# Four chained graph layers on one core: the new-state gate's state side as seven block products, SiLU as one ScalarE function, and a schedule search with other durations

## The chip, the cores and the metric

The kernel runs on one core of a Trainium2 chip. The metric is the device time of one execution in microseconds (us), taken as the median of several executions. All data are float32. The core has one engine for matrix products (TensorE, "PE" in the profile; its weight loads are shown apart as "PEld"), three engines for elementwise work (VectorE "DVE", ScalarE "ACT", GpSimd "POOL") and a queue for transfers (SyncE "SP"). The engines run beside each other and wait for one another by semaphores.

## The reference, cut to what matters

The input x has 128 graphs of 64 nodes with 256 features. Four layers follow one another; each adds its result to x and normalises the sum.

```python
def gru(m, h):                                    # layer 0, five rounds
    gi, gh = m @ w_ih.T + b_ih, h @ w_hh.T + b_hh
    r = sigmoid(i_r + h_r); z = sigmoid(i_z + h_z)
    n = tanh(i_n + r * h_n)                       # n: the candidate; h_n: state's side of it
    return (1 - z) * n + z * h
for l in range(5):
    agg = A.T @ (h @ weight[l]);  h = gru(agg, h)
x = layernorm(x + h * mask)

agg = epsilon * x + adj @ x                       # layer 1
hid = silu(rmsnorm(agg @ W1 + b1) * rms_weight)
x = layernorm(x + hid @ W2 + b2)

x = layernorm(x + project(expmap0(adj @ logmap0(x))))   # layer 2: artanh (a logarithm), tanh

h = x @ W_w.T + W_b; a = softmax-like(exp(h @ a1 + h @ a2) * adj)   # layer 3
x = layernorm(x + a @ h)
```

## The kernel before: the parts that the change and the steps touch

The 128 graphs are taken in 16 groups of 8 (`NG = 16`), so a group has 512 columns of features (`R = 512`), cut in two halves of 256 (`HR = 256`). The 256 features are two blocks of 128 (`KD = 2`), one for each set of 128 partitions. All instructions of all groups are first only listed, each with an engine, an assumed duration and what it reads and writes. A search (`Flow`, `Plan`) then plays several orders through, with up to four groups under way at once, keeps the best plan, and issues the instructions in that order. Some copies may go to either ScalarE or VectorE (`either`, `copied`, `scaled`); the search picks the engine. The order on each engine is then fixed, and the chip's engines wait for semaphores where the plan's times do not hold.

One round of layer 0 for one group:

```python
def sides(n):                                      # for each half n
    ...                                            # transposes of h, aggregate -> agg (p_agg)
    p_hn = bank("p_hn")
    product(p_hn, w_hn, lambda k: h[:, k, half(n)], True, True, (h, n))   # 4 matmuls of 256 columns
    for c in range(KD):                            # evict with the bias, either engine
        scaled(300, hnb[:, c, half(n)] <- p_hn[:, c*HR:(c+1)*HR], 0.5, half_b...)

sides(0)
product(p1, a11[l], agg half 0); copied(420, uu <- p1)
product(p_in[0], w_in[l], agg half 0)
product(p1, a12, h half 0); tanh_half(ur <- p1)
new_n(0, ur)
p_a2 = sides(1)
minus(t1, a2, of(a, 0)); minus(t2, of(h, 1), t1)    # 4 VectorE instructions, 128x512
minus(t3, of(h, 1), a2); minus(t4, t2, of(h, 0))
product(pu, s2[l], t2); plus(uu, pu, uu)
product(pv, s3[l], t3); plus(uv, pv, uu)
product(pw, s1[l], t1); product(pv, na22, t4); plus(uv, pw, uv); plus(uz, pv, uu)
product(pw, s4[l], h half 1); ...
product(p_in[1], w_in[l], agg half 1); ...
```

The gates r and z for both halves are a 2x2 by 2x2 product of blocks (blocks: agg or h, gate r or z, half 0 or 1). It is done with seven block products in place of eight: `a11`, `a12`, `s1` to `s4`, `na22` are sums and differences of weight blocks, `t1` to `t4` those of the data. A block product here is four matmuls. The candidate's two sides, `w_in` on agg and `w_hn` on h, are plain: eight matmuls each for both halves.

Layer 1's activation, with `half_r` half of `rms_w` and `w2s` scaled by `rms_w` once at the start:

```python
for c in range(KH):                                # 8 chunks of 128x512 in each group
    dve: v = (v + b1) * ps_r
    act: th = tanh(half_r * v)
    dve: v = (th + 1) * v
```

The search's assumptions:

```python
pe:  {512: 0.86, 256: 0.435, 128: 0.23, 1: 0.21} us
dve: 0.16 + 0.00105 * n    act: 0.27 + 0.00077 * n     pool(us)
act(2600, ... AF.Ln ...)                           # the logarithm with its table loads, as a long operation
```

Of the kernel before, what the change touches and what calls it, by code (L numbers as in the profile page):

```python
# [16 lines left out]
P = 128  # L17
# [25 lines left out]
class Op:  # L43
    __slots__ = ("eng", "us", "run", "ways", "stream", "n", "kb", "need", "then", "bufs", "opens", "id", "way")

    def __init__(self, ways, stream, n, kb):
        self.ways = {eng: (us, run) for eng, us, run in ways}
        self.eng, self.us, self.run = ways[0]
        self.stream, self.n, self.kb = stream, n, kb
        self.need, self.then, self.bufs, self.opens, self.id, self.way = 0, [], (), None, 0, 0.0  # L50


class Plan:


    def __init__(self, flow):
# [10 lines left out]
        self.past, self.order = None, []  # L67

    def copy(self):
# [6 lines left out]
        c.past, c.order = (self.past, self.order), []  # L76
        return c

    def advance(self, until, rank):
# [3 lines left out]
        while self.left and clock["PE"] < until:  # L83
            best = None
            for s in range(self.first, min(self.first + flow.WINDOW, len(self.queues))):
                for e, q in self.queues[s].items():
                    opened = False
                    for _, o in zip(range(flow.AHEAD[e]), q):
# [10 lines left out]
                        key = (t + o.ways[e][0] - min(w[0] for w in o.ways.values()) if len(o.ways) > 1 else t, *rank(s, o))  # L99
# [4 lines left out]
            _, o, eng, t = best  # L104
            for e in o.ways:
                self.queues[o.stream][e].remove(o)
# [37 lines left out]
class Flow:  # L144
# [13 lines left out]
    HOPS = {"from PE": 0.25, "to PE": 0.3, "else": 0.1}  # L158
# [3 lines left out]
    TRANSFERS = 8  # L162
    WINDOW, STRETCH, WIDTH, LAG = 4, 25.0, 8, 40.0
# [13 lines left out]
    def op(self, eng, us, run, w=(), r=(), kb=0):  # L177
        self.either([(eng, us, run)], w, r, kb)

    def either(self, ways, w, r, kb=0):  # L180

        o = Op(ways, len(self.streams) - 1, len(self.ops), kb)
# [31 lines left out]
    def hop(self, e, to):  # L214
        if e == to:
            return 0.0
        return self.HOPS["from PE" if e == "PE" else "to PE" if to == "PE" else "else"]

# [42 lines left out]
def kernel(  # L261
# [82 lines left out]
    def act(n, run, w, r):  # L344
        flow.op("ACT", 0.27 + 0.00077 * n, run, w, r)
# [72 lines left out]
    def gate_w(name):  # L418
        return fixed([P, KD, D], name)

    a12, na22, w_hn = gate_w("a12"), gate_w("na22"), gate_w("w_hn")
    a11, s1, s2, s3, s4, w_in = ([gate_w(f"{n}_{l}") for l in range(L)] for n in ("a11", "s1", "s2", "s3", "s4", "w_in"))
# [6 lines left out]
    half_b, half_r = fixed([P, NV], "half_b"), fixed([P, KH], "half_r")  # L429
# [36 lines left out]
    flow.op("ACT", 1.5, lambda: nc.scalar.activation(warm, one4, AF.Tanh))  # L466
# [23 lines left out]
    dve(4, lambda: nc.vector.tensor_scalar(half_r.tile(), cols[:, 2 * NV + KH:], 0.5, None, OP.mult), [half_r], [cols])  # L490
# [13 lines left out]
    def hh_out(i, k, ps):  # L504
        if i == 0:
            dve(256, lambda: nc.vector.tensor_copy(a12[:, k, :], ps[:, :D]), [(a12, k)], [ps])
            dve(256, lambda: nc.vector.tensor_scalar(na22[:, k, :], ps[:, D:], -1.0, None, OP.mult), [(na22, k)], [ps])
        else:
            dve(256, lambda: nc.vector.tensor_copy(w_hn[:, k, :], ps[:, :D]), [(w_hn, k)], [ps])
# [10 lines left out]
    for l in range(L):  # L520
# [9 lines left out]
        a21 = unit("AB"[l % 2], S, f"a21_{l}", (P, KD, D))  # L530
        for k in range(KD):
            for i, n in ((0, 2 * D), (1, D)):
# [5 lines left out]
                for dst, at in (((a11[l], 0), (a21, D)) if i == 0 else ((w_in[l], 0),)):  # L538
                    act(256, lambda ps=ps, k=k, dst=dst, at=at: nc.scalar.copy(dst[:, k, :], ps[:, at:at + D]),
                        [(dst, k)], [ps])  # L540

        def sums(e, us, l=l, a21=a21):
            v = nc.vector if e == "DVE" else nc.gpsimd
            for o, x0, x1 in ((s1[l], a21, na22), (s2[l], s1[l], a11[l]), (s3[l], a11[l], a21), (s4[l], a12, s2[l])):
                flow.op(e, us, lambda o=o, x0=x0, x1=x1: v.tensor_sub(o.tile(), x0.tile(), x1.tile()), [o], [x0, x1])
        sums("DVE", 0.7) if l == 0 else sums("POOL", 1.32)
# [5 lines left out]
    m11, m12, mn22, ms1, ms2, ms3, ms4 = range(7)  # L552
# [34 lines left out]


    for k in range(KH):
        act(256, lambda k=k: nc.scalar.activation(w2s[:, k, :], w2s[:, k, :], AF.Identity, scale=rmsc(k)), [(w2s, k)], [(w2s, k), cols])  # L590
# [21 lines left out]
    def group(g):  # L612
# [104 lines left out]
        def gated(l, h):  # L717
# [5 lines left out]
            def sides(n):  # L723
# [5 lines left out]
                p_agg = aggregate(agg, hr, 2 * n, n)  # L729
                p_hn = bank("p_hn")  # L730
                product(p_hn, w_hn, lambda k: h[:, k, half(n)], True, True, (h, n))
                for c in range(KD):
                    scaled(300, lambda c=c: hnb[:, c, half(n)], lambda c=c: p_hn[:, c * HR:(c + 1) * HR], lambda: 0.5,
                           lambda c=c: half_b[:, 2 * KD + c:2 * KD + c + 1], [(hnb, (n, c))], [p_hn, half_b])
                return p_agg
# [3 lines left out]
            t1, t2, t3, t4 = (tA, 0), (tA, 1), (tB, 0), (tB, 1)  # L739
            a = agg  # L740

            def view(t):
                return t[0][:, t[1] * KD:(t[1] + 1) * KD, :]

            def minus(o, x0, x1, r):
                dve(512, lambda: nc.vector.tensor_sub(view(o), x0(), x1()), [o], r)  # L746

            def of(t, n):
                return lambda: t[:, :, half(n)]

            def k_of(t, n):
# [351 lines left out]
```

## Time and profile before

| | before |
|---|---|
| time, median of 3 (lowest to highest) | 2431.12 us (2430.6 to 2432.45) |
| span of the profiled execution | 2430.5 us |
| PE busy | 2394.7 us, 12258 matmul records |
| PEld busy | 2102.9 us |
| DVE busy | 1893.4 us |
| ACT busy | 1147.1 us |
| POOL busy | 188.2 us |
| HBM traffic | 25.74 MB read, 8.39 MB written |

A line of the profile's groups reads: source line, engine, operation, what it writes and reads by the program's names, shapes, the number of records; then the busy time in us and the mean duration of one in ns; then the time for which the engine stood idle just before such instructions, and who ended that. One float32 matmul instruction leaves two records: `p_hn`, for instance, has 16 x 5 x 8 = 640 instructions in the program and 1280 records. As matmuls overlap in the pipeline, the mean duration of one record is longer than the distance between two.

### The profile page before, as it was taken

Reading aid. Unit: us, or ns where it says so; the run is one execution under the profiler, and the core shown is the slowest. Engines: PE = TensorE matmul, PEld = TensorE weight load, DVE = VectorE, ACT = ScalarE, POOL = GpSimd, SP = SyncE. Lnnn points to the kernel's source line nnn. Section 1 sums busy time; section 2 is a strip of 40 time slices with the busy share of each in tenths; the row PEclk is TensorE's granted clock in tenths of the full one; section 3 lists DMA queues with packets and bytes.
Section 4 is the critical chain, followed back from the end, with each engine's and each line's share of the span. In section 5 each row is a group of like instructions: output and inputs, shape, how many; then the busy total and the mean of one; then the engine's idle time right before and its main releaser. Section 6 shows DMA issues by size and latency. Waiting matters only on the chain.

```text
span 2430.5 us, 32703 instructions
## 1 busy us (share of the span) xinstructions
PE 2394.7 (99%) x12258; PEld 2102.9 (87%) x12258; DVE 1893.4 (78%) x4097; ACT 1147.1 (47%) x2408; POOL 188.2 (8%) x144
## 2 busy tenths in 40 slices
PE   9999999999999999999999999999999999999995
PEld 7888888888888888888888888888888888888864
DVE  3668787887888877778777887888787787878777
ACT  4434544444444444454444545455444544445453
POOL 4000000000100000000000100000000000000011
PEclk9999999999999999999999999999999999999997
DMA  4000000000000000000000000000000000000000
GB/s 127 3 1 12 1 29 1 18 12 1 29 1 27 3 18 11 1 27 3 16 14 1 29 1 27 3 19 11 1 29 1 18 12 1 27 9 18 9 9 18
DMA packets 39725, 36.21 MB, mean 15 GB/s; under 512 B 9956, under 2 KB 38656, under 8 KB 39568
## 3 DMA queue, kind: packets, MB, share of 16 engines
q1 hardware_dynamic: 37840, 32.25, 4.2%
q8 instruction: 97, 1.59, 0.3%
q10 hardware_dynamic: 1328, 1.31, 0.2%
q0 software_dynamic: 400, 0.57, 0.1%
q14 instruction: 60, 0.49, 0.1%
HBM read 25.74 MB, written 8.39 MB: 14 GB/s over the span
## 4 chain that ended last, share of the span: by engine, by line
PE 94%; DVE 4%; ACT 1%; DMA 1%; issue 0%; POOL 0%; SPq 0%; POOLq 0%; ACTq 0%; DVEq 0%
PE p_v L663 11%; PE p_w L663 11%; PE p_in L663 11%; PE p_r L663 11%; PE p_hn L663 11%; PE ps_o L333 9%; PE ps_agg L333 6%; PE p_u L663 6%; PE ps_hr L643 3%; PE ps_a L333 2%; PE p_wh L882 2%; PE p_vh L882 2%; PE p_1h L882 2%; PE ps_T L633 1%; PE ps_att L333 1%; PE p_uh L882 1%
## 5 line engine op out<-in xcount | busy, mean ns | idle before, releaser
L663 PE MATMUL p_hn<-hT,w_hn 128*128 128x256 f32 x1280 | 322.8, 380 | 0.0
L663 PE MATMUL p_in<-agg,w_in 128*128 128x256 f32 x1280 | 315.4, 379 | 0.0
L663 PEld LDWEIGHTS p_in<-agg,w_in 128*128 128x128 f32 x1280 | 240.2, 190 | 31.1
L663 PEld LDWEIGHTS p_hn<-hT,w_hn 128*128 128x128 f32 x1280 | 227.9, 191 | 22.7
L333 PE MATMUL ps_o<-w2s,hid 128*128 128x256 f32 x1024 | 231.2, 379 | 0.0
L333 PEld LDWEIGHTS ps_o<-w2s,hid 128*128 128x128 f32 x1024 | 193.9, 190 | 27.3 <-issue 1.2
L678 POOL TENSOR_TENSOR rstd<-ve,pow 128x4 f32<-128x4 f32 (+1 forms) x64 | 82.5, 1289 | 1491.6 <-DVE ve L676 1484.0
L767 ACT ACTIVATE V<-V,half_b 128x256 f32<-128x256 f32 x160 | 72.7, 500 | 199.2 <-DVE V L763 199.0
L663 PE MATMUL p_u<-tA,s 128*128 128x256 f32 x640 | 158.1, 381 | 1.4 <-DVE tA L746 0.6
L663 PE MATMUL p_w<-tA,s 128*128 128x256 f32 x640 | 158.1, 379 | 0.0
L663 PE MATMUL p_r<-hT,a 128*128 128x256 f32 x640 | 156.9, 379 | 0.0
L663 PE MATMUL p_r<-agg,a 128*128 128x256 f32 x640 | 156.7, 379 | 0.0
L663 PE MATMUL p_v<-tB,s 128*128 128x256 f32 x640 | 155.4, 379 | 0.0
L663 PE MATMUL p_v<-tB,na 128*128 128x256 f32 x640 | 154.5, 379 | 0.0
L663 PE MATMUL p_w<-hT,s 128*128 128x256 f32 x640 | 154.3, 379 | 0.0
L349 ACT COPY agg<-ps_agg 128x512 f32<-128x512 f32 x154 | 89.9, 584 | 114.2 <-PE ps_agg L333 98.8
L333 PEld LDWEIGHTS ps_agg<-edge,hr 128*128 128x128 f32 x1024 | 136.1, 191 | 6.6
L354 ACT ACTIVATE hnb<-p_hn,half_b 128x256 f32<-128x256 f32 x232 | 101.6, 472 | 81.4 <-PE p_hn L663 67.4
L333 PE MATMUL ps_agg<-edge,hr 128*128 128x128 f32 x1024 | 138.8, 275 | 0.0
L663 PEld LDWEIGHTS p_u<-tA,s 128*128 128x128 f32 x640 | 119.3, 190 | 21.0 <-DVE tA L746 2.3
L663 PEld LDWEIGHTS p_v<-tB,s 128*128 128x128 f32 x640 | 120.9, 190 | 16.3 <-PE ps_att L333 0.2
L663 PEld LDWEIGHTS p_w<-hT,s 128*128 128x128 f32 x640 | 120.7, 190 | 16.0
(233 smaller groups left out, 4686.5 us busy)
## 6 DMA issues: line engine op xcount, KB each, us to landing
x<-in_x_dram SPq DMA_DIRECT2D x16, 512.0 KB, 3.6
xr<-in_x_dram SPq DMA_DIRECT2D x16, 512.0 KB, 3.6
out_dram<-x_n SPq DMA_DIRECT2D x16, 512.0 KB, 2.9
edge<-in_adj_dram SPq DMA_DIRECT2D x32, 64.0 KB, 2.3
wm<-in_L_gnn_weight_dram SPq DMA_DIRECT2D x5, 256.0 KB, 5.3
w2s<-in_L_gnn_W_dram SPq DMA_DIRECT2D x1, 1024.0 KB, 10.0
w<-in_L_gnn_W_dram SPq DMA_DIRECT2D x2, 512.0 KB, 3.5
w_in_L_gnn_w_hh_dram<-in_L_gnn_w_hh_dram ACTq DMA_DIRECT2D x1, 512.0 KB, 5.2
```

What stands on the lines that cost most here:

```text
L333: return nc.tensor.matmul(o, lhsT, rhs, start=(k == 0), stop=(k == nk - 1))
L349: flow.either([("ACT", 0.27 + 0.00077 * n, lambda: nc.scalar.copy(o(), i())), ("DVE", 0.16 + 0.00105 * n, lambda: nc.vector.tensor_copy(o( ...
L354: flow.either([("ACT", 0.27 + 0.00077 * n, lambda: nc.scalar.activation(o(), i(), AF.Identity, bias=bias(), scale=scale())), ("DVE", 0.16 ...
L633: turn(lambda j=j, c=c: nc.tensor.transpose(ps[:, c * HR + j * P:c * HR + (j + 1) * P], src[:, 2 * n + j, c * P:(c + 1) * P], ident.tile() ...
L643: turn(lambda j=j, c=c: nc.tensor.transpose(ps[:, j * D + c * P:j * D + (c + 1) * P], src[:, c, (2 * n + j) * P:(2 * n + j + 1) * P], iden ...
L663: pe(256, lambda c=c, k=k: nc.tensor.matmul(ps[:, c * HR:(c + 1) * HR], w[:, k, c * P:(c + 1) * P], v(k), start=first and c == k == 0, sto ...
L678: pool(1.1, lambda: nc.gpsimd.tensor_tensor(rstd[:, :m, :], ve[:, :m, :], pow2[:, :m, :], OP.pow), [rstd], [ve])
L767: act(256, lambda c=c: nc.scalar.activation(o[:, c, :], src(c), AF.Tanh, bias=half_b[:, i * KD + c:i * KD + c + 1], scale=0.5), [(o, c)], ...
L882: pe(256, lambda c=c: nc.tensor.matmul(ps[:, c * HR:(c + 1) * HR], w1f[:, w, (2 * q + c) * P:(2 * q + c + 1) * P], v[0](), start=first and ...
```

## The change

There are three parts.

**State's side of the candidate.** `h @ w_hn` for both halves is itself made a 2x2 by 2x2 product (blocks: input features 0 or 1, output features 0 or 1, half 0 or 1) with seven block products, each of one matmul of 256 columns. It needs the four data sums `t1` to `t4` of h over features and halves. So that the gates can share them, the gates' product is cut in the same way: its blocks are now input features 0 or 1, and each block product takes h's part and agg's part one after the other into the same bank (`gate`). The sums are now made for h and for agg apart, each 128x256.

```diff
-            def sides(n):
+            def agg_of(n):
                 ...
-                p_hn = bank("p_hn")
-                product(p_hn, w_hn, lambda k: h[:, k, half(n)], True, True, (h, n))
-                for c in range(KD):
-                    scaled(300, lambda c=c: hnb[:, c, half(n)], ...)
+            def sums(x, i):
+                for o, x0, x1 in ((of(t1), at(0, 1), at(0, 0)), (of(t2), at(1, 1), of(t1)),
+                                  (of(t3), at(1, 1), at(0, 1)), (of(t4), of(t2), at(1, 0))):
+                    dve(256, ... nc.vector.tensor_sub(o[0](), x0[0](), x1[0]()) ...)
+            def gate(ps, m, v, first, last):
+                for i, w in ((1, w_h), (0, w_a[l])):
+                    for c in range(KD):
+                        pe(256, ... nc.tensor.matmul(ps[:, c * HR:(c + 1) * HR], w[:, m, c * P:(c + 1) * P], v[i][0](), ...))
+            def state_side():
+                px, py = bank("p_hx"), bank("p_hy")
+                prod(px, 0, m11, block(0, 0), True)
+                copied(256, su[0], lambda: px[:, :HR], ...)
+                prod(px, 0, m12, block(1, 0))
+                scaled(256, out(0, 0)[0], lambda: px[:, :HR], lambda: 1.0, lambda: b(0), ...)
+                prod(px, 1, ms2, sum_of(t2));        plus(su, px, 1, su)
+                prod(py, 0, ms3, sum_of(t3), True);  plus(sv, py, 0, su)
+                prod(py, 1, ms1, sum_of(t1))
+                prod(py, 0, mn22, sum_of(t4))
+                plus(out(0, 1), py, 0, su, 1);       plus(out(1, 1), py, 1, sv, 1)
+                prod(py, 1, ms4, block(1, 1));       plus(out(1, 0), py, 1, su, 0)
...
-            sides(0)
-            product(p1, a11[l], k_of(a, 0), True, False, (a, 0))
+            agg_of(0)
+            gate(p1, m11, block(0, 0), True, False)
             copied(420, lambda: uu.tile(), lambda: blocks_of(p1.tile()), [uu], [p1])
-            product(p_in[0], w_in[l], k_of(a, 0), True, True, (a, 0))
-            product(p1, a12, k_of(h, 0), False, True, (h, 0))
+            gate(p1, m12, block(1, 0), False, True)
             tanh_half(ur, ...)
+            sums(h, 1)
+            state_side()
+            product(p_in[0], w_in[l], lambda k: agg[:, k, half(0)], True, True, (agg, 0))
             new_n(0, ur)
-            p_a2 = sides(1)
-            minus(t1, ...); minus(t2, ...); minus(t3, ...); minus(t4, ...)
-            product(pu, s2[l], k_view(t2), True, True, t2)
+            agg_of(1)
+            sums(agg, 0)
+            gate(pu, ms2, sum_of(t2), True, True)
             plus(uu, pu, uu)
             ...                                    # pv, pw in the same way
```

The weights' sums are made once at the start, in the same blocks (`w_h`, `w_hn`, and `w_a` for each round); for rounds 1 to 4 on GpSimd as before.

**Layer 1's activation.** ScalarE's SiLU function takes the place of the tanh and of one VectorE instruction, and the scaling of `w2s` at the start goes.

```diff
-            th = u("VZR"[c % 3], f"th{c}")
-            act(512, ... nc.scalar.activation(th.tile(), v, AF.Tanh, scale=half_r[:, c:c + 1]) ...)
-            dve(512, ... nc.vector.scalar_tensor_tensor(v, th.tile(), 1.0, v, OP.add, OP.mult) ...)
+            act(512, lambda v=v, c=c: nc.scalar.activation(v, v, AF.Silu, scale=rmsc(c)), parts, [*parts, cols], SILU)
...
-    for k in range(KH):
-        act(256, ... w2s[:, k, :] = w2s[:, k, :] * rmsc(k) ...)
```

**The search.** It now knows which function tables ScalarE holds (`sets`: tanh with exp or with SiLU, exp, the logarithm and SiLU each in their own), adds a load where the table changes, prefers ScalarE for a copy that either engine can take unless VectorE is earlier by a margin, and has some other durations.

```diff
+    TANH, EXP, LN, SILU = ("exp", "silu"), ("exp",), ("ln",), ("silu",)
+    TABLE = 1.28
+    SOONER = 0.4
+                        elif o.sets and self.table not in o.sets:
+                            t += flow.TABLE
-                        key = (t + o.ways[e][0] - min(w[0] for w in o.ways.values()) if len(o.ways) > 1 else t, *rank(s, o))
+                        key = (t + flow.SOONER if len(o.ways) > 1 and e == "DVE" else t, *rank(s, o))
-    HOPS = {"from PE": 0.25, "to PE": 0.3, "else": 0.1}
+    HOPS = {"from PE": 0.25, "to PE": 0.3, "else": 0.1, "own": 0.0}
-        act(2600, lambda: nc.scalar.activation(fac.tile(), fac.tile(), AF.Ln), [fac], [fac])
+        act(4, lambda: nc.scalar.activation(fac.tile(), fac.tile(), AF.Ln), [fac], [fac], LN)
-        dve(800, onto_ball, [th, un], [th, un, urn])
+        dve(900, onto_ball, [th, un], [th, un, urn])
```

## Prediction

> **What bounds the kernel now.** I read the shares of the engines first, then the slices, then PE's waits stretch by stretch, and last the chain of work that ended last. The page opens with these lines:
>
> ```profile
> PE 2394.7 (99%) x12258; PEld 2102.9 (87%) x12258; DVE 1893.4 (78%) x4097; ACT 1147.1 (47%) x2408; POOL 188.2 (8%) x144
> PE   9999999999999999999999999999999999999995
> DVE  3668787887888877778777887888787787878777
> PE 94%; DVE 4%; ACT 1%; DMA 1%; issue 0%; POOL 0%; SPq 0%; POOLq 0%; ACTq 0%; DVEq 0%
> ```
>
> PE is busy in every slice but the last, and 94% of the chain is PE. A table by stretches (span, then PE, PEld, DVE, ACT and POOL busy) tells where its 35.8 us of idle time lie:
>
> ```profile
> 0.00:61.00 61.00, 57.60 (x277) 43.77 (x278) 21.80 (x54) 24.86 (x60) 26.23 (x32) 1.00 0.43 127
> ...
> 2300.00:2370.00 70.00, 66.03 (x270) 45.51 (x270) 52.65 (x90) 38.84 (x68) 8.57 (x5) 0.98 0.03 8
> 2370.00:2431.00 61.00, 34.97 (x146) 28.33 (x144) 46.80 (x188) 23.80 (x58) 10.01 (x8) 0.77 0.05 18
> 300.00:2300.00 2000.00, 1997.29 (x10343) 1773.35 (x10342) 1600.54 (x3441) 953.30 (x2001) 134.73 (x93) 1.00 0.04 13
> ```
>
> The start leaves 3.4 us, the last 130 us leave 29.5, and the 2000 us in between only 2.7, although VectorE has 80% of that stretch to do. So in the middle time is PE work and nothing else; at the end it is a chain of small operations. The unit of PE work is read from the timeline, where groups of eight records (four instructions) of 256 columns begin 1.72 to 1.73 us apart:
>
> ```profile
> 1212.05 1.89 PE L663 MATMUL p_u<-tA,s 128*128 128x256 f32 x8
> 1213.77 1.89 PE L663 MATMUL p_v<-tB,s 128*128 128x256 f32 x8
> 1215.50 1.03 PE L663 MATMUL p_w<-tA,s 128*128 128x256 f32 x4
> ```
>
> One matmul instruction of 256 columns is therefore 0.432 us, not the 380 ns of a record's mean, as records overlap.
>
> **What the Trainium skill says.** "Perfetto Trace Analysis", section "Identifying the Most-Contended Engine", warns that matmul busy time is a bad measure of the distance to the roofline, as pipelined matmuls look smaller, and points to the weight loads' share. Here that is 87% and the distance between matmuls is steady, so I count instructions by their distance. "ScalarE: Activation LUTs", section "What happens when an `exp` ACTIVATE runs", says that the time per element is the same for every function; by that SiLU should cost what tanh does, 720 ns for 128x512 in this trace (no SiLU has run here yet). Its section "What ACT_TABLE_LOAD costs" gives 1283 ns for a load, which the trace shows to the nanosecond, and about 1380 ns of drain beside it, which the trace does not show: the load at 2382.99 us is followed by its logarithm at 2384.29. "VectorE: DVE Perf Modes", section "The TRN2 errata — SBUF-src ops pay a fixed extra latency per instruction", says that many small tiles pay a fixed cost each. The trace agrees: 128x256 differences take a median of 418 to 425 ns, 128x512 ones 681 to 742, so two halves cost some 0.84 us where one whole costs about 0.71.
>
> **The change part by part.** I compared the two instruction streams, engine by engine; counts below are from them, durations from the trace before.
>
> *State's side.* In each group and round, eight matmuls become seven: 16 x 5 = 80 fewer of 256 columns (4508 to 4428); no other PE count moves. The gates keep 28 matmuls a round. 80 x 0.432 = **34.6 us** of PE work go, all in the stage where PE is the path.
>
> *VectorE.* Removed: the four wide differences per round (59.4 + 57.9 + 54.9 + 54.5 = 226.7 us), SiLU's second half (82.8), 88 evictions of p_hn (41.4), and work that the search now gives to ScalarE: 88 normalised rows of y, 36 of xb, 32 tangents, 31 copies of hr and 26 of hw, at their busy time apiece 32 + 13 + 9 + 21 + 13 = 88. Sum 439. Added: 640 differences of 128x256 at 0.42 = 269, 160 additions from PSUM at 0.42 = 67 and 240 with a bias at 0.48 = 115 (the sizes of the rows that add xb and y from PSUM). Sum 451. Net **+12 us on 1893**, so VectorE stays at 78 to 80%. All of it lies beside PE.
>
> *ScalarE.* Removed: 232 evictions of p_hn (102) and the scaling of w2s (4). Added: 78 copies and 78 biased copies of p_hx (about 30 + 37), the work from VectorE (124 x 0.55 + 32 x 0.5 + 31 x 0.58 + 26 x 0.47 = 114), and 17 more table loads, 48 in place of 31, at 1.283 = 22. Net **about +97 us on 1147**, some 51%: a filler, not a bound. These are my sums of mean durations.
>
> *Waits in the middle.* PE had only these waits between 61 and 2300 us:
>
> ```profile
> PE p_uh L882 <- DVE t L878: 1.4, 4, 0.6
> PE p_u L663 <- DVE tA L746: 0.6, 1, 0.6
> PE p_u L663 <- ACT junk_a L1006: 0.5, 1, 0.5
> ```
>
> The new state side has longer hand-overs (copy p_hx, then add into the same half bank; three chained additions), but other groups' matmuls stand between its products in the stream. I allow **+1 us**.
>
> *The start.* The first round needs w_hn's four sums and h's sums before most of state's side, where before p_hn could run straight from w_hn and h. In the stream those products are mixed with small transposes, so I allow **+1 us** on 3.4.
>
> *The end.* Here the order counts. Before, groups 14 and 15 go through layer 1 together: 14's ps_o matmuls fill the hole in which 15 waits for its norm. In the changed stream, 14's ps_o are all issued ahead of 15's sixteen ps_hid, and between those and 15's ps_o there stand only 15's ps_ss, four ps_sup of 14 and four transposes, about 3.1 us of PE work. The chain through that hole, with durations from the trace: copy 0.6 + square 0.7 + sum 0.7 + ps_ss 0.8 + ms 0.2 + root on GpSimd 1.2 + transposes 0.5 + scaling 0.75 + SiLU 0.7, with some 1.5 of hand-overs, is 7.7; SiLU's table load, which is queued behind 14's tangents and squares, brings it to about 9. That is **+6 us** of new idle time. Against it: the old hole before ps_hid (2.5) and the one before ps_hr (1.4) are filled by 14's ps_o, about −1.5; and after 15's last ps_o VectorE has less left, 30 us of small operations in place of 40 by the same durations, because 14 is a norm ahead. Before, the path from the last ps_o (2384.1) to the end took 46.4 us:
>
> ```profile
> 2387.74 2.51 PE L333 MATMUL ps_sup<-tan,adjT 128*128 128x256 f32 x8 [3.65 <-ACT tan L995]
> 2393.24 3.75 PE L333 MATMUL ps_sup<-tan,adjT 128*128 128x256 f32 x8 [3.00 <-DVE tan L994]
> 2402.30 1.97 PE L633 MATMUL ps_T<-ident,x_n 128*128 128x128 f32 x8 [5.30 <-ACT x_n L354]
> ```
>
> PE waits there for one group's small chain at a time. Only part of VectorE's 10 us is on the path; I take 3 us off the span after ps_o, of which 1.7 is PE work that moved ahead, so −1. Together the end gives back **+3.5 us**.
>
> Sum: 2431.1 − 34.6 + 1 + 1 + 3.5 = **2402.0 us**, 1.2% less.
>
> **The rivals.** *VectorE becomes the bound.* For it: 306 more instructions (4094 to 4400), many short. Against: the busy sum moves by 12 us only, and at 80% PE waited 2.7 us in 2000. If 1% of the middle went to such waits, 2425. *The new hand-overs stall PE.* For it: a half bank is read and then added to, 160 hand-overs more; if each showed 0.2 us, 32 us would come back and nothing be gained, 2430. Against: four groups under way and a search that counts these hops. *The end gets better, not worse.* The search orders for the end and knows table loads now; if the hole is filled by what I overlooked, the idle time falls by some 8 us in place of rising: 2388. *Table loads disturb.* 17 more loads beside half-idle ScalarE should cost nothing; each that did would cost 1.3, at most 22 us.
>
> **Range and chances.** The 34.6 us are sure to 0.5 us as PE work. The idle time is uncertain: from 8 less to 16 more than before around my +5.5, hence 2390 to 2413. More than 2% faster needs 2382.5, that is 14 us of idle time removed beyond the matmuls: unlikely, 0.04. Slower by 2% needs stalls of 80 us: 0.01.
>
> **What would show it.** Matmul records 160 fewer (12258 to about 12098) and PE busy near 2360 us; VectorE 1890 to 1920 us; ScalarE near 1245 with 48 table loads; SiLU near 720 ns. PE's waits from 300 to 2300 us below 5 us; a wait of 5 to 7 us at the first ps_o of the last group, and 40 to 45 us from its last ps_o to the end. I am wrong if waits of p_hx or p_hy on ACT or DVE add up to more than 10 us, if VectorE passes 85% in the middle, or if a 256-column matmul's distance is no longer 0.432 us.

## The result, and the profile after

The changed kernel takes **2460.86 us** (median of four runs, 2459.38 to 2462.58) against 2431.07 us: 1.0122 times as long, 95% interval 1.0104 to 1.0139. It is slower by 29.8 us; 2402.0 us had been forecast, 29.1 less than before, and the range of 2390 to 2413 us does not hold it.

The opening lines of its page, in the same order as those of before (busy time of the engines, VectorE's slices, engines of the chain that ended last):

```profile
PE 2391.6 (97%) x12098; PEld 2071.1 (84%) x12098; DVE 1898.5 (77%) x4403; ACT 1220.4 (50%) x2552; POOL 172.6 (7%) x144
DVE  5678778788688867877777788878868878878665
PE 87%; DVE 8%; ACT 3%; DMA 1%; issue 1%; POOL 0%; POOLq 0%; SPq 0%; ACTq 0%; DVEq 0%
```

The 160 matmul records are gone, yet PE's busy time fell by 3 us in place of 35, and PE has only 87% of the chain, with VectorE and ScalarE at 11% where they had 5%. The table by stretches (span, then PE, PEld, DVE, ACT and POOL busy) shows where:

```profile
0.00:61.00 61.00, 57.59 (x276) 43.68 (x277) 33.67 (x88) 21.37 (x49) 17.04 (x30) 1.00 0.40 124
300.00:2300.00 2000.00, 1966.34 (x10072) 1720.11 (x10071) 1589.55 (x3673) 1017.48 (x2135) 131.22 (x96) 1.00 0.04 13
```

The first 61 us are as before (57.59 us of PE against 57.60). The 2000 us in the middle, which had 2.7 us without PE, have 33.7, and they hold 10072 records in place of 10343. PE's waits in that stretch (us in total, times, longest) name the instructions at line 783, which are the products of state's side:

```profile
PE p_hy L783 <- DVE hnb L794: 6.6, 29, 0.9
PE p_hx L783 <- DVE tA L759: 6.5, 3, 2.2
...
PE p_hx L783 <- ACT hnb L365: 2.3, 12, 0.2
...
PE p_hy L783 <- DVE tA L759: 1.0, 1, 1.0
```

These are 16.4 us, over the 10 us that the prediction named as its refutation. But they don't make up 30, and 7.5 of them are waits for `tA`, the sums of h, not for a reader of the bank. A matmul record that starts late is drawn longer (483 ns in place of 379 in the stall below), so part of a stall is counted as busy. So I measured it from starts: for each record the distance from the start of the one before it, less the steady distance (216 ns for 256 columns, two records to an instruction; 110 ns for 128; 430 for 512). I call the sum *excess*, here and below. It holds everything that PE loses: waits, weight loads that no longer overlap, half clock.

| us | excess to 300 | 300 to 2300 | of it before `p_hx`, `p_hy`/`p_hn` | from 2300 | sum |
|---|---|---|---|---|---|
| before | 4.9 | 8.4 | 0.7 | 23.9 | 37.2 |
| after | 7.5 | 63.9 | 35.7 | 30.9 | 102.3 |

The account closes: 65.1 us more excess less 34.6 us of matmuls is +30.5, and +29.8 were measured. That is bookkeeping, as the distances between starts add up to the time whatever PE waits for; it shows where the time goes and that the steady distances held, not why. In the middle of the changed kernel 72 records have an excess of 0.15 to 0.4 us (21.2 us together) and 11 one of over 1 us (18.8 us). Before had 4 and none.

One of the 72, from the timeline (start, duration, engine, line, operation; in brackets the idle time before and who ended it):

```profile
353.08 1.03 PE L783 MATMUL p_hy<-tA,w_hn 128*128 128x256 f32 x4
...
354.15 0.42 DVE L792 TENSOR_TENSOR hs<-p_hy,hs 128x256 f32<-128x256 f32 x1 [1.90 <-PE p_hy L783]
...
354.38 0.59 PE L772 MATMUL p_w<-tB,w_a 128*128 128x256 f32 x2
354.61 0.48 DVE L794 SCALAR_TENSOR_TENSOR hnb<-p_hy,half_b,hs 128x256 f32<-128x256 f32 x1
...
355.15 0.30 PEld L783 LDWEIGHTS p_hy<-tA,w_hn 128*128 128x128 f32 x2 [0.58 <-DVE hnb L794]
355.15 0.70 PE L783 MATMUL p_hy<-tA,w_hn 128*128 128x256 f32 x2 [0.17 <-DVE hnb L794]
```

A bank of PSUM, the memory that matmuls write, holds both halves of `p_hy`, 2 x 256 columns. The four records at 353.08 are the products `ms3` into half 0 and `ms1` into half 1 of `p_hy`. Then VectorE reads half 0 (`hs`, done at 354.57) and half 1 (`hnb`, done at 355.09). The product at 355.15 is `mn22`, which adds to **half 0**. Half 0 was free at 354.57, in time for PE, whose next slot was 354.38 + 0.43 = 354.81. But the product and its weight load waited for the reader of half 1, and 0.34 us were lost. The plan lists the halves as separate buffers (`(ps, 0)`, `(ps, 1)`); the built program's semaphores guard the whole bank. Counted in the program, 144 of the 560 products of state's side wait for a reader of the other half.

Laid beside the trace, product by product, these waits say what the 35.7 us are. Between 300 and 2300 us, 120 products wait in the program for a reader of the other half, and 33.9 us of the excess lie at them; at four of the 120, with 7.9 us, a sum of h in `tA` came later still, each time after VectorE had waited 2.5 to 4.5 us for the previous group's output to leave the same slot (`tA` from `DMA out_dram`). So some 26 us are the guard's alone. The 52 products whose wait is for a reader of the same half have 0.0 us.

That guard isn't an excess of caution. The Trainium skill, "PSUM — Partial Sum Buffer", section "PSUM bank collisions raise a hardware error", says that engines which touch one bank in the same partitions at once collide even at different columns, and to guard by bank and quadrant, not by address. No run here tries a collision; that the program guards so, the timeline shows.

### The profile page after: what moved, and what is told of

It reads as the page before. It is cut to its first block, busy times and chain, and to the rows that moved or that the text cites. A ratio compares the mean times of both kernels' runs of the same rounds, so it can differ in the third digit from the quotient of the medians.

```text
span 2459.0 us, 32880 instructions
## 1 busy us (share of the span) xinstructions
PE 2391.6 (97%) x12098; PEld 2071.1 (84%) x12098; DVE 1898.5 (77%) x4403; ACT 1220.4 (50%) x2552; POOL 172.6 (7%) x144
## 4 chain that ended last, share of the span: by engine, by line
PE 87%; DVE 8%; ACT 3%; DMA 1%; issue 1%; POOL 0%; POOLq 0%; SPq 0%; ACTq 0%; DVEq 0%
PE p_w L772 11%; PE p_v L772 10%; PE p_r L772 10%; PE p_in L675 9%; PE ps_o L342 8%; PE ps_agg L342 6%; PE p_hy L783 6%; PE p_u L772 5%; PE p_hx L783 4%; PE ps_hr L655 3%; PE ps_a L342 2%; PE p_vh L938 2%; PE p_wh L938 2%; PE p_1h L938 2%; PE ps_sup L342 1%; DVE hnb L794 1%
## 5 line engine op out<-in xcount | busy, mean ns | idle before, releaser
L675 PEld LDWEIGHTS p_in<-agg,w_in 128*128 128x128 f32 x1280 | 241.4, 191 | 33.7 <-ACT agg L360 2.1
L342 PEld LDWEIGHTS ps_o<-w2s,hid 128*128 128x128 f32 x1024 | 193.5, 191 | 30.9 <-ACT hid L998 5.5
L772 PE MATMUL p_r<-hT,w_h 128*128 128x256 f32 x640 | 167.9, 381 | 2.6 <-ACT U L360 2.3
L772 PE MATMUL p_v<-tA,w_h 128*128 128x256 f32 x640 | 168.6, 380 | 1.6 <-DVE V L822 1.6
L772 PE MATMUL p_r<-agg,w_a 128*128 128x256 f32 x640 | 166.9, 381 | 0.5 <-ACT agg L360 0.5
L772 PE MATMUL p_v<-tB,w_a 128*128 128x256 f32 x640 | 166.4, 379 | 0.0
L794 DVE SCALAR_TENSOR_TENSOR hnb<-p_hy,half_b,hs 128x256 f32<-128x256 f32 x240 | 109.7, 480 | 60.6 <-PE p_hy L783 57.8
L783 PE MATMUL p_hy<-tA,w_hn 128*128 128x256 f32 x480 | 136.1, 390 | 6.8 <-DVE hnb L794 5.5
L772 PEld LDWEIGHTS p_r<-agg,w_a 128*128 128x128 f32 x640 | 120.7, 191 | 17.9 <-ACT agg L360 1.7
L772 PEld LDWEIGHTS p_v<-tB,w_a 128*128 128x128 f32 x640 | 120.8, 190 | 16.0
L772 PEld LDWEIGHTS p_r<-hT,w_h 128*128 128x128 f32 x640 | 118.2, 191 | 17.9 <-ACT U L360 2.9
L772 PEld LDWEIGHTS p_v<-tA,w_h 128*128 128x128 f32 x640 | 116.4, 190 | 15.8 <-DVE V L822 2.8
```

The source lines that it names most:

```text
L342: return nc.tensor.matmul(o, lhsT, rhs, start=(k == 0), stop=(k == nk - 1))
L675: pe(256, lambda c=c, k=k: nc.tensor.matmul(ps[:, c * HR:(c + 1) * HR], w[:, k, c * P:(c + 1) * P], v(k), start=first and c == k == 0, sto ...
L772: pe(256, lambda i=i, w=w, c=c: nc.tensor.matmul(ps[:, c * HR:(c + 1) * HR], w[:, m, c * P:(c + 1) * P], v[i][0](), start=first and i == 1 ...
L783: pe(256, lambda: nc.tensor.matmul(ps[:, j * HR:(j + 1) * HR], w_hn[:, m, :], v[1][0](), start=first, stop=True, skip_group_check=True), [ ...
L794: dve(300, lambda: nc.vector.scalar_tensor_tensor(o[0](), ps[:, j * HR:(j + 1) * HR], b(c), x[0](), OP.add, OP.add), [o[1]], [(ps, j), x[1 ...
```

## The experiments

Every kernel was timed beside the kernel before. Ratios are to that one (95% interval). "State's side" is the excess from 300 to 2300 us before `p_hx` and `p_hy` (or `p_hn`). Three numbers of the search are edited: its sight (how many operations ahead it looks in each queue of VectorE and ScalarE, 10 in the changed kernel), its width (how many plans it keeps, 8) and its stretch (it plans in pieces of 25 us). After every edit it draws up a new plan, so no two rows have the same order of instructions.

| run | what | us | ratio | excess 300–2300 | state's side | from 2300 |
|---|---|---|---|---|---|---|
| e1 | changed, plan told whole bank | 2449.90 | 1.0081 (1.0064–1.0097) | 55.5 | 14.6 | 29.6 |
| e2 | e1, products ordered by bank | 2431.85 | 1.0002 (0.9993–1.001) | 30.9 | 7.2 | 36.4 |
| e3 | changed, plain state's side | 2441.66 | 1.0044 (1.0029–1.0059) | 14.0 | 0.2 | 30.0 |
| e4 | before + SiLU + search | 2440.83 | 1.0039 (1.0024–1.0054) | 12.5 | 0.6 | 31.0 |
| e5 | before + SiLU | 2436.61 | 1.002 (1.0012–1.0028) | 12.3 | 1.0 | 25.6 |
| e6 | before + search | 2434.85 | 1.0012 (1.0005–1.0019) | 11.8 | 0.5 | 22.8 |
| e7 | changed, a bank per half | 2450.84 | 1.0083 (1.0068–1.0098) | 58.2 | 13.9 | 30.4 |
| e8 | e2, output's transfer known | 2431.05 | 0.9998 (0.999–1.0007) | 37.4 | 2.1 | 29.7 |
| e9 | e2, output in h's slots | 2424.79 | 0.9971 (0.9961–0.9982) | 32.9 | 2.3 | 29.6 |
| e10 | e9, sight of 20 operations | 2414.09 | 0.9927 (0.9911–0.9944) | 23.5 | 0.6 | 25.6 |
| e11 | e9, 24 plans | **2405.48** | 0.9893 (0.9878–0.9908) | 17.3 | 3.3 | 23.7 |
| e12 | e9, VectorE not held back | 2454.29 | 1.0093 (1.0078–1.0109) | 56.7 | 7.1 | 30.3 |
| e14 | changed, 24 plans | 2446.43 | 1.0052 (1.0037–1.0067) | 54.2 | 38.1 | 24.9 |
| e15 | before, 24 plans | 2429.97 | 0.9992 (0.9984–1.0001) | 7.6 | 0.6 | 24.0 |
| e16 | e9, 24 plans and sight of 20 | 2413.93 | 0.9927 (0.9912–0.9942) | 20.8 | 3.8 | 29.8 |
| e17 | changed, stretches of 24 us | 2454.09 | 1.0088 (1.0071–1.0104) | 58.8 | 25.9 | 30.4 |
| e18 | e9, stretches of 24 us | 2429.78 | 0.9992 (0.9983–1.0001) | 34.7 | 0.9 | 31.9 |
| e19 | before, stretches of 24 us | 2429.41 | 0.999 (0.9983–0.9997) | 8.4 | 0.5 | 20.3 |

In every row before's time plus the added excess, less 34.6 us where the seven products are used, gives the measured time within 3 us, as it must while the steady distances hold.

### Is it the bank?

e1 gives the plan the whole bank for every access and keeps the order of the products:

```diff
-                        [(ps, 0), (ps, 1)] if first else [(ps, j)], [(w_hn, m), v[1][1]])
+                        [ps], [(w_hn, m), v[1][1]])
...                        # likewise [ps] for (ps, j) and (px, 0) in every reader
```

> Only the search's bookkeeping differs from the changed kernel: for p_hx and p_hy it is told that every product and every reader touches the whole bank, not one half of it, which is how the built program's semaphores treat them. Theory 1 (the search planned on halves that the semaphores do not keep apart, so PE runs into waits it had not planned): PE's excess before p_hx and p_hy between 300 and 2300 us, 35 us now, falls below 8 us, and the time to 2408 to 2428 us. Theory 2 (the hand-overs between PE and VectorE simply take longer than assumed, whatever the bookkeeping): the excess stays at 20 us or more and the time at 2445 to 2462. Theory 3 (not the state side, but SiLU's table loads and the copies moved to ScalarE): no difference, 2455 to 2463.

e2 adds an order in which two products fill both halves, then both are read, then the next two follow:

```diff
                 prod(px, 0, m12, block(1, 0))
-                scaled(256, out(0, 0)[0], ...)
                 prod(px, 1, ms2, sum_of(t2))
+                scaled(256, out(0, 0)[0], ...)
                 plus(su, px, 1, su)
                 prod(py, 0, ms3, sum_of(t3), True)
-                plus(sv, py, 0, su)
                 prod(py, 1, ms1, sum_of(t1))
-                prod(py, 0, mn22, sum_of(t4))
-                plus(out(0, 1), py, 0, su, 1)
+                plus(sv, py, 0, su)
                 plus(out(1, 1), py, 1, sv, 1)
+                prod(py, 0, mn22, sum_of(t4))
                 prod(py, 1, ms4, block(1, 1))
+                plus(out(0, 1), py, 0, su, 1)
                 plus(out(1, 0), py, 1, su, 0)
```

> As e1_whole_bank, and the seven products are put in another order, so that both halves of a bank are written in one go and then both are read: m11; copy; m12 and ms2; two readers; ms3 and ms1; two readers; mn22 and ms4; two readers. Theory 1: four hand-overs of a bank in place of six or seven, excess before p_hx and p_hy below 5 us, time 2398 to 2418 us, below e1_whole_bank and below the kernel before. Theory 2: fewer hand-overs help in proportion, 2435 to 2450. Theory 3: 2450 to 2463.

e7 leaves the products' order in the list alone and gives each half a bank:

```diff
-                px, py = bank("p_hx"), bank("p_hy")
+                px, px1, py, py1 = bank("p_hx"), bank("p_hx1"), bank("p_hy"), bank("p_hy1")
```

> The changed kernel with one edit: each half of p_hx and p_hy gets a PSUM bank of its own (four banks in place of two for state's side), product order as in the changed kernel. Theory (144 products wait for a reader of the other half of their bank, which a bank apiece makes impossible): PE's excess before the records of state's side falls from 35.7 to below 12 us, and the time from 2461 to about 2435 to 2442 us. Rival (the waits come from the reads of the same half and from the chain of additions; banks do not matter): state's side keeps over 25 us and the time stays above 2452. A third outcome: four of eight banks held at once make other work wait for banks; then the excess before state's side falls, but that before other products rises by as much.

In all three the excess before state's side falls: 35.7 to 14.6, 7.2 and 13.9 us. PE's waits of `p_hy` for `hnb` (29 times, 6.6 us) are gone from the middle in each. So the false wait is real, and a bank per half takes it away with no other edit to what is computed (a new plan comes with it). But e1 and e7 gained only 11 and 10 us, because the excess elsewhere rose from 28 to 41 and 44 us. e7 is nearest to the third outcome that was named; that the banks held at once are what does it was not tested apart, and e1, which holds two banks as before, rose by nearly as much. The order by bank turns it into time: e2 is 29.0 us faster than the changed kernel and level with before. Theory 1 was too hopeful in both: it had put e1 at 2408 to 2428 us and e2 at 2398 to 2418 us. The guard explains the excess before state's side, not the whole loss. The waits on PE that are then largest in its middle are of another kind:

```profile
PE ps_o L342 <- ACT hid L998: 3.0, 2, 2.7
PE p_v L772 <- DVE V L822: 3.0, 2, 1.7
PE p_hx L783 <- DVE tA L759: 2.7, 2, 1.4
PE p_hy L783 <- DVE tA L759: 2.1, 2, 1.1
```

They are few and long, where the changed kernel had many and short. I read them as chains that come late as a whole; no run shows that apart.

### The other parts of the change

e3 is the changed kernel with the eight plain products of before for state's side (`p_hn`, evictions with the bias); e4 is the kernel before with SiLU and the search's new assumptions.

> The changed kernel with state's side of the candidate as the plain eight products per round and group again (two banks, each written in one go and evicted with the bias); the gates' new cut, SiLU and the search stay. Theories 1 and 2 (state's side is what costs): the 80 matmuls come back, 34.6 us, and the waits go, so 2428 to 2442 us with PE's idle time from 300 to 2300 us near 5 us. Theory 3: 2460 or more, with idle time from 300 to 2300 us near 30 us.

> The kernel before with two of the three parts: SiLU in layer 1 and the search's new assumptions; gates and state's side as before. Theories 1 and 2: nothing is lost, 2426 to 2437 us, PE's idle time from 300 to 2300 us below 8 us. Theory 3: 2450 us or more, as these parts then cause the loss.

Against before, SiLU and search cost 9 us (e4, 2440.8 us, between the ranges of the theories), the gates' new cut 1 us more (e3 less e4), and state's side 19.2 us (after less e3): the 34.6 us of matmuls are saved and 54 us of excess come with it. Each is the difference of two plans, so the 1 us means nothing. e5 and e6 take e4 apart:

```diff
-            act(512, ... AF.Tanh, scale=half_r[:, c:c + 1]) ...; dve(512, ... (th + 1) * v ...)
+            act(512, lambda v=v, c=c: nc.scalar.activation(v, v, AF.Silu, scale=rmsc(c)), parts, [*parts, cols])
```

> The kernel before with one thing of the change alone: layer 1's activation as one ScalarE SiLU (no tanh, no second half on VectorE, no scaling of w2s); search, gates and state's side are those of before. The search still counts no table loads. Theory (the 9 us of the version with SiLU and the new search assumptions come from the changed hand-over at the end: SiLU sits on the last group's path with its table load): 2433 to 2441 us, with the excess beyond 300-2300 us grown by 3 to 8 us and the middle below 12 us of waits. Rival (SiLU is neutral or a gain, as it takes 83 us off VectorE; the search's assumptions cost the 9 us): 2428 to 2432 us.

e6 has the search's part of the change alone, with the tanh of before.

> The kernel before with the search's new assumptions alone (shorter durations, no bonus for the faster engine, VectorE held back by 0.4 us where ScalarE can do it, table loads counted); no SiLU, same products. Theory (SiLU at the end is what costs): 2430 to 2434 us. Rival (the search's assumptions cost it, by another order at the end or by work pushed to ScalarE): 2437 to 2441 us, with 3 to 5 us more of waits of PE on ACT in the middle or 5 us more at the end.

SiLU alone costs 4.4 us, the search's assumptions alone 2.6. Neither is where my theory put it: SiLU's excess rose by 3.9 us in the middle, where ps_o waits five times for it, and by 1.7 at the end; the end's 7 us appear only with both. Differences of these sizes are within what another plan gives (below), so I don't explain them further.

### Is it the output's transfer?

In the changed kernel and in e2, VectorE's first sum of h waits 20.7 and 17.1 us in total for the previous group's output to leave the same slot. e8 tells the search of the transfer, e9 moves the tile:

```diff
-        flow.op("SP", 0.1, lambda: nc.sync.dma_start(out_rows[g], o.tile()), (), [o])
+        flow.op("SP", 0.1, lambda: nc.sync.dma_start(out_rows[g], o.tile()), (), [o], kb=512)     # e8
-        o = layer_norm(y3, "A", "n3")
+        o = layer_norm(y3, "h", "n3")                                                             # e9
```

> The version ordered by bank (2431.9 us), with one number more: the search is told that the output's transfer moves 512 KB, so it counts its landing some 4.5 us after the issue, where before it took it to be over in 0.1 us. The tile of the output shares its slot with the sums of h in the same group slot. Theory (a part of the 31 us of waits that are left in the middle comes from the sums of h waiting for that transfer, 17 us of VectorE's time): the waits of tA on the output's DMA fall from 17 us to below 3, PE's excess in the middle falls by 8 to 15 us, 2417 to 2425 us. Rival (VectorE has slack enough, its waits there do not reach PE; what is left comes from 80% busy VectorE and short hand-overs): the waits vanish and the time stays within 2 us of 2432.

> The version ordered by bank (2431.9 us), with the output's tile in the slots of h (two buffers, next written after layer 0's gates of the following group) in place of the slot that the sums of h want first; the search's numbers stay. Theory (waits of the sums of h for the output's transfer reach PE): no wait of tA on the output's DMA, PE's excess in the middle falls by 8 to 15 us, 2417 to 2425 us, as in the run where the search knows the transfer. Rival (those waits cost PE nothing): within 2 us of 2432. If this one gains and the one with the known transfer does not, planning around the transfer costs as much as the wait.

The waits vanish in both, and my theory fell for this version: the middle's excess went from 30.9 to 37.4 and 32.9 us, not down by 8 to 15. What e9 gained (7 us) lies in the end's excess, 36.4 to 29.6, which the theory does not explain. The excess before state's side did fall, from 7.2 to 2.1 and 2.3 us, but as much and more came back before other products. So the waits did not set the sum; how much of that is the new plan was not tested. In the changed kernel itself such waits reached PE with the 7.9 us above.

### Is it the search?

e10, e11 and e16 change its sight (`AHEAD`) and its width (`WIDTH`); e12 takes back the margin by which VectorE is held off work that ScalarE can do:

```diff
-    AHEAD = {"PE": 32, "DVE": 10, "ACT": 10, "POOL": 4, "SP": 2}
+    AHEAD = {"PE": 32, "DVE": 20, "ACT": 20, "POOL": 4, "SP": 2}       # e10, e16
-    WINDOW, STRETCH, WIDTH, LAG = 4, 25.0, 8, 40.0
+    WINDOW, STRETCH, WIDTH, LAG = 4, 25.0, 24, 40.0                    # e11, e16; e14 and e15 on after and before
-    SOONER = 0.4
+    SOONER = 0.0                                                       # e12
```

> The version ordered by bank with the output's tile in h's slots (2424.8 us, 33 us of waits left in the middle), with one edit in the search: it may look 20 operations ahead in each stream's queue for VectorE and ScalarE, in place of 10. State's side with its sums is nine dependent VectorE operations in a row, so that a window of 10 sees little beyond it. Theory (the waits left come from this short sight): PE's excess in the middle falls from 33 to below 22 us, 2410 to 2417 us. Rival (what is left is timing that the search does not foresee): within 4 us of 2425.

> The same version (2424.8 us) with a search that keeps 24 plans in place of 8 at each stretch. Theory (the search finds no better order with these numbers because it keeps too few): excess below 25 us in the middle and less at the end, 2412 to 2420 us. Rival (its plans are already free of waits by its own count, and the chip differs from that count): within 5 us of 2425, either way.

> The same version (2424.8 us) with VectorE no longer held back by 0.4 us where ScalarE can do the work too. Theory (work handed to the slower ScalarE lengthens the chains that PE waits for at the end, where ps_T waits 6.5 us for a normalised row on ScalarE): the end's excess falls from 29.6 to about 25 us, 2418 to 2422 us, VectorE's busy time rises by about 80 us. Rival (VectorE at 80% in the middle is what makes PE wait, so more work on it costs): the middle's excess rises by over 5 us, 2428 to 2440 us.

> The version ordered by bank with the output's tile in h's slots, with both edits of the search that helped it: 24 plans (2405.5 us) and 20 operations of sight for VectorE and ScalarE (2414.1 us). Theory (both take away waits that come from the longer chains, and the excess in the middle can fall to the 8 us of the kernel before): excess of 10 to 15 us in the middle, 2396 to 2403 us. Rival (they find the same gain, the rest is timing that the search does not count): 2403 to 2408 us.

With 24 plans the version by bank takes 2405.48 us, 1.1% less than before, the fastest of all and better than its theory had it (2412 to 2420 us). Its middle stretch:

```profile
300.00:2300.00 2000.00, 1990.62 (x10295) 1761.46 (x10294) 1616.31 (x3731) 1041.13 (x2172) 131.67 (x96) 1.00 0.04 13
```

9.4 us without PE, where the changed kernel had 33.7, and VectorE does more in the same time (1616 us against 1590). Sight of 20 gained 10.7 us with 8 plans, but on top of 24 plans it lost 8.5 (e16, 2413.9 us, outside both ranges), mostly at the end (23.7 to 29.8 us). So its gain does not add to that of the width, and it may be that of one plan. e12 is the opposite of what my theory had it; its rival was right and too small (2428 to 2440 us). e9's engines, then e12's:

```profile
PE 2374.6 (98%) x12098; PEld 2076.6 (86%) x12098; DVE 1899.9 (78%) x4405; ACT 1222.1 (50%) x2550; POOL 172.9 (7%) x144
PE 2373.7 (97%) x12098; PEld 2075.4 (85%) x12098; DVE 1988.3 (81%) x4605; ACT 1131.8 (46%) x2347; POOL 170.4 (7%) x144
```

88 us of work moved to VectorE cost 29.5 us, with the middle's excess up from 32.9 to 56.7. VectorE at 81% of the span is still not busy all the time, yet more work on it came with more waits of PE; before's 80% in the middle had cost 2.7 us. This is one plan, far outside what another plan gave.

### Or the luck of one plan?

Each edit gives the search another order. e17, e18 and e19 cut the plan in stretches of 24 us in place of 25, which means nothing; e14 and e15 give 24 plans to the changed kernel and to before.

> The changed kernel (2461 us) with one number edited: the search keeps 24 plans in place of 8. The halves of a bank are still planned as independent, the product order and the output's slot are those of the changed kernel. Theory (what the search cannot see, no number of plans mends: 144 products wait for readers of the other half): PE's excess before state's side stays above 20 us and the time above 2440 us. Rival (the loss is only a poor plan out of many): 2405 to 2425 us, as the version ordered by bank with 24 plans (2405.5 us).

> The kernel before (2432 us) with the search keeping 24 plans in place of 8. Theory (before has 8.4 us of excess in the middle, so there is little to find; only the end's 24 us can move): 2424 to 2432 us, so that most of the 20 us that the same edit gave the version ordered by bank belong to that version's longer chains. Rival (a wider search is worth 20 us to any version): 2408 to 2416 us.

> The changed kernel with an edit that means nothing: the search cuts its plan in stretches of 24 us in place of 25, so it finds another order by the same rules. It tells how far the time moves with the order alone. Theory (the loss is in what is computed and how it is guarded, in every plan): 2448 to 2470 us, over 25 us of excess before state's side. Rival (2461 us was an unlucky plan): below 2440 us.

> The version ordered by bank with the output's tile in h's slots (2424.8 us), 8 plans, with the meaningless edit of the search (stretches of 24 us). It tells how far this version moves with the plan alone. The changed kernel moved by 7 us with it, the kernel before by under 3. Theory (its chains are longer than those of before, but no wait is hidden from the search): within 10 us of 2425, below the 2440 to 2461 us of every version that plans half banks. Rival (the gain of the order was luck): above 2435 us.

> The kernel before with the same meaningless edit, stretches of 24 us in place of 25. Theory (before has slack enough that any plan serves): 2428 to 2436 us, and the difference between kernels is not luck of the plan. Rival (plans differ by 15 us and more whatever the kernel): outside 2420 to 2444 us.

All five fell within the ranges of their theories. The meaningless edit moved the changed kernel by −6.8 us, e9 by +5.0 and before by about −2.6. So I take nothing under 8 us for an effect, a bound that rests on one such edit to each of three kernels. Above it stand: the order by bank (−29.0 us with 8 plans; −41.0 from e14 to e11 with 24, the output's slot included), the width (−14.4 on the changed kernel, −19.3 on e9, −2.0 on before) and the margin for VectorE (e12). In the changed kernel's three plans state's side keeps 25.9 to 38.1 us of excess. With 24 plans (e14) both kinds of wait are still there, the late sums in the first line, five of the six after a wait for the output, and the bank's guard in the second:

```profile
PE p_hx L783 <- DVE tA L759: 11.7, 6, 2.2
PE p_hy L783 <- DVE hnb L794: 4.7, 21, 0.5
```

Counted as above, the guard alone costs 26 us in the changed kernel, 21 in e14 and 20 in e17. 24 plans did not mend what the search cannot see. In the eight versions by bank the excess before state's side is 0.6 to 7.2 us.

## Why the prediction was wrong, point by point

- **What bounds the kernel**: PE still has 87% of the chain that ended last. But "in the middle time is PE work and nothing else" was a finding about before's plan, and was carried over: of the changed kernel's middle 63.9 us are excess.
- **34.6 us of matmuls**: right. 160 records are gone (12098), and the steady distance of a 256-column record is 216 ns in both kernels.
- **VectorE +12 us, ScalarE +97**: 1898.5 (+5) and 1220.4 (+73, so 24 less than forecast); 48 table loads of 1283 ns, SiLU 713 ns for 128x512 where 720 was expected. That SiLU would cost what tanh does held. One reading was off without weight: 742 ns for a 128x512 difference is a mean; the medians are 681 to 691.
- **Waits in the middle +1 us**: this is the step that failed. It was +55.5 us (8.4 to 63.9). The reason given, that other groups' matmuls stand between the products and that the search counts the hops, assumed that the search knows what each product waits for. I read the half bank in the plan's list and did not look which semaphores the built program has. 35.0 of the 55.5 us stand before state's side, some 26 of them by the guard and 7.9 by sums of h that came late after the output's transfer, which the search took to be over at once.
- **The rival "the new hand-overs stall PE"** named the right place and the wrong hand-over, with 32 us at 0.2 us for each of 160 and 2430 us. That the excess before state's side, 35.7 us, is near 32 is luck: the hand-overs within one half, which it counted, cost 0.0 us at the 52 products that wait for them, and the cost sits at the other half's reader. The other 20 us of the middle no rival had. 6 of them are there with the plain state's side too (e3: 14.0 less 0.2, against before's 8.4 less 0.7), and 24 plans took 12 off them in the changed kernel (28.2 to 16.1); that longer chains, harder to order, are the cause is argued, not shown.
- **The rival "VectorE becomes the bound"**: not in the changed kernel, whose VectorE has 1590 us to do in the middle, less than before. But the argument against it (PE waited 2.7 us at 80%) does not carry over to another set of chains, as e12 suggests.
- **The start +1 us**: +2.6 by excess, to 300 us. **The end +3.5**: +7.0 by excess, twice the forecast. The hole of some 6 us is there, in two pieces:

```profile
PE ps_o L342 <- ACT hid L998: 3.2, 1, 3.2
PE ps_ss L342 <- DVE sqs L926: 2.2, 1, 2.2
```

From the last `ps_o` (2414.7 us) to the end are 44.3 us, within the 40 to 45 that were forecast.

What stays open: why e1's and e7's other waits rose as state's side's fell; what the 9 us of excess are that e11 still has over before in the middle; and the end's excess, which goes from 20.3 to 36.4 us from plan to plan.

## What to carry to other kernels

Before you save matmuls by adding into half a PSUM bank, count who else touches that bank. Here the other half's reader was a wait, so fill both halves, read both, then go on, and tell a planner the bank, not the half. Measure PE's loss by the distance between starts, as busy time hid some 25 of 55 us here. And where a search orders the program, time a meaningless edit first: differences below what it moves (here 3 to 7 us) are no verdict on a change.

## What the runs showed of the hardware that was not expected

In the changed kernel PE's clock drops to half for 3.41 us, twice in the middle of the run. In the two stretches of 5 us that hold them (the clock is the third number from the end):

```profile
395.00:400.00 5.00, 4.76 (x14) 3.94 (x15) 3.15 (x9) 0.00 (x0) 0.00 (x0) 0.66 0.01 3
740.00:745.00 5.00, 4.30 (x14) 3.51 (x15) 4.52 (x19) 3.90 (x9) 0.00 (x0) 0.66 0.01 2
```

Half clock for 3.41 of 5 us is 0.66, and no such stretch stands in the middle of before, which has its first after the start at 2338 us. The first stretch begins 0.9 us after PE had been idle for 2.1 us; three other idle times of 2.2 to 2.7 us brought none. The second begins at 740.9 us, after idle times of 0.9 and 1.2 us within the 3 us before it. The Trainium skill, "TensorE: Matmul & The Clock Gate", section "HAM oscillation — how this bites in real kernels", puts the rule at no idle gaps over about 3.4 us; in this trace half clock followed shorter ones, and what decides between those that bring it and those that don't stays open. Each stretch costs at most 1.7 us (half of 3.41), so the two are at most 3.4 of the middle's 63.9 us of excess and not the cause.
